# Two x tiles move into bytes that attention's far pool frees early, and stay until layer 2; the last pieces of layer 1 are split

## The chip, the cores and the metric

The kernel runs on one core of a Trainium2 chip. TensorE (PE) multiplies matrices, VectorE (DVE), ScalarE (ACT) and GpSimd (POOL) work on tiles in the on-chip memory SBUF or in the matmul accumulators (PSUM), and transfers between SBUF and the main memory (HBM) are issued from the queue of an engine: here that of SyncE (SP), or now and then that of ScalarE or GpSimd. Each engine works through its instructions in order and waits on semaphores for others. The metric is the device time of one execution in microseconds (us).

## The reference

A residual network of four layers on x of shape (1, 256, 256, 128) in float32, that is 65,536 tokens of 128 channels. Each layer gets the group-normalised x and its output is added to x:

```python
x = x + attention(gn(x))            # layer 0: triangle attention, 4 heads of 32 channels, pair bias
x = x + multiply16(gn(x))           # layer 1:
#   a = sigmoid((x@Wa1+ba1) * (x@Wa2+ba2)); b likewise, 16 channels each
#   z = einsum("bikc,bkjc->bijc", a, b)
#   out = sigmoid(x@Wg+bg) * (layernorm(z)@Wz + bz)
x = x + multiply128(gn(x))          # layer 2: zn = layernorm(x); a, b, k with 128 channels
#   out = sigmoid(zn@Wgo+bgo) * (layernorm(k)@Wlo + blo)
x = x + conv(gn(x))                 # layer 3: small convolutions and shifts
```

The group normalisation before a layer (gn0 to gn3) needs the mean and the variance of the whole x, 32 groups of four channels. So no layer can start before the last piece of the x before it is summed up.

## The kernel before

x lies channel by channel in HBM: 128 partitions by 65,536 tokens. The versions after each layer are called xT, x1T, x2T and x3T. Outside attention they are worked on in 32 tiles (NSC) of 2,048 tokens (SC), 1 MB each. Parts of the kernel are written with the order of instructions fixed by hand (manual_schedule); between the parts the instructions of one engine follow one another in the order of the program, or as the planner places them.

**Attention (layer 0)** works on 64 groups (NG) of 1,024 tokens (GT = 4 rows of 256). A loop over j (L700) takes half a group at a time: it loads x of the group after next (load_x, L482) and its normalising factors (load_rs, L487), centres and scales them to xn (centre, L496; prepare), projects xn of the next group to q, k, v and the gate (project, L514 to L536), computes the scores of this group (L545, each matmul reads a slice of k and one of q), adds the bias and takes exponentials (weigh, L559 on), multiplies with v (attend, L578), and, two or three groups later, divides, projects out (output) and writes x1T (close, L636; the store L641 is on SyncE's queue, those of the last two groups on ScalarE's). Its SBUF pools: p2, which rotates two tiles of q, k and xn each, three of v, the gate and u, and five of x; p2e for the exponentials, and p2c for the bias.

**Between the layers.** order1 (L776) is the order of the tiles in layer 1. Thirteen pools of one tile each (slots) are opened once attention's pools are closed, over the same bytes. Eight loads (FIRST, L786) are issued on SyncE's queue. gn1's statistics are merged (L790), a flag tells whether a number has overflowed (L791 to L799), the flag is read into a register of every engine (L800), and under tc.If (L801) a general attention would be computed anew and the eight tiles loaded again; this branch isn't taken. Then gn_groups (L194 to L208) turns the statistics into a mean and 1/sqrt(variance) for each channel: two small matmuls, a square root on ScalarE (L206) and a reciprocal. The factors are folded into the weights (L824 to L832).

**Layer 1.** p3 (L846 to L880) first issues the loads of slots 8 to 12 (L853), then for each tile eight matmuls (L860), an activation (L869), a product (L870), a sigmoid (L846) and the store of 0.25 MB to abD; the next load takes the slot that the tile left (load1 at L784). z (L883 to L941) multiplies a and b. p4 (L944 to L1030) takes the tiles in another order, beginning with the last twelve, which are still in the slots: gate4 computes the gate, TensorE the projection of z into PSUM (pz, one tile's two halves at a time), VectorE the product (L1008), and the sum is added to x, on GpSimd (L1019) for most tiles and on VectorE (L1015) for those of by_dve, where the product is left in PSUM until it is added. sum4 (L979 to L981) squares the new tile on ScalarE and sums it, and the tile is stored to x2T from SyncE (L1025, the last one L1030).

**Layer 2.** x_pool (x57) holds seven tiles. gn2 (L1041 to L1065) sums up the statistics and folds them in as gn1 did. load5 (L1090) loads x2 tiles, the first four on GpSimd's queue, the others on SyncE's; square5, sums5 and root5 compute the layer norm's factors, the first tile by itself; the factors of each tile go through a row in HBM (rs2D). Then each tile goes through five products (L1154), the gated a and b are stored to aD and bD, and p6, p7 and p9 follow.

Of the kernel before, what the change touches and what calls it, by code (L numbers as in the profile page):

```python
# [16 lines left out]
P = 128  # L17
N = 256
# [14 lines left out]
def kernel(ctx: ExitStack, tc: tile.TileContext, a: dict, out: bass.AP):  # L33
# [435 lines left out]


    stats1 = new_stats("stats1")
    rzD = dram.tile([N // 4, 16, N], F32, name="rzD")
# [3 lines left out]
    with tc.tile_pool(name="p2e", bufs=6, reuse_waits="tile") as eb, tc.tile_pool(name="p2c", bufs=1, reuse_waits="tile") as cs:  # L476
        triT = cs.tile([P, NH, 2, N], F32, name="triT")
        with tc.tile_pool(name="p2", bufs=2, reuse_waits="tile") as sb, tc.tile_pool(name="p2S", bufs=2, space=PSUM, reuse_waits="tile") as psS, tc.tile_pool(name="p2z", bufs=1, space=PSUM, reuse_waits="tile") as psZ, tc.tile_pool(name="p2M", bufs=3, space=PSUM, reuse_waits="tile") as psM, ExitStack() as by_hand:
            groups = {}
            rows = {}  # L480

            def load_x(g):  # L482
                x = sb.tile([P, GT], F32, name="p2_x", bufs=5)
                nc.sync.dma_start(x, xT[:, g * GT : (g + 1) * GT])
                groups[g] = dict(x=x)
# [10 lines left out]
            def centre(g):  # L496
                t = groups[g]
                t["xn"] = sb.tile([P, GT], F32, name="p2_xn")
                nc.scalar.activation(t["xn"], t["x"], AF.Identity, bias=mneg)  # L499
                return t["xn"]  # L500
# [5 lines left out]
            def tiles(g):  # L506
                t = groups[g]
                t["q"] = sb.tile([P, GT], F32, name="p2_q")
                t["k"] = sb.tile([P, GT], F32, name="p2_k")
                t["v"] = sb.tile([P, GT // P, D], F32, name="p2_v", bufs=3)  # L510
                t["g"] = sb.tile([P, GT], F32, name="p2_g", bufs=3)
                t["u"] = sb.tile([P, GT], F32, name="p2_u", bufs=3)
# [190 lines left out]
            for j in range(2 * NG + 5):  # L703
# [5 lines left out]
                if not 0 <= out[0] < NG:  # L709
                    out = None  # L710
                if j == 20:

                    pick = cs.tile([P, G, P], F32, name="pick")
                    nc.gpsimd.tensor_copy(
                        pick.rearrange("p r (h m) -> p r h m", h=NH),
                        ident.rearrange("p (h x) -> p x h", h=NH)[:, 0:G, :].unsqueeze(3).to_broadcast([P, G, NH, HC]),
                    )

                    nc.sync.dma_start(
                        sD_tap[:, 8:].rearrange("k (h w) -> k h w", w=NP)[:, :, 0:8],  # L720
                        fill[:, 0:1, :].to_broadcast([TAPS, N + 2, 8]),
                    )
                    nc.sync.dma_start(sD_tap[:, 0:8], fill[:, 0, :])
                    nc.sync.dma_start(
                        sD_tap[:, 16 : 8 + NP].rearrange("k (a w) -> k a w", w=8),
                        fill[:, 1:2, :].to_broadcast([TAPS, N // 8, 8]),
                    )
                    nc.sync.dma_start(
                        tD[:, NP : 2 * NP].rearrange("o (a w) -> o a w", w=8),
                        fill[0:1, 0:1, :].to_broadcast([1, NP // 8, 8]),  # L730
                    )
# [43 lines left out]

    order1 = [b + h * NSC // 2 for b in range(NSC // 2) for h in range(2)]  # L776
    SLOTS, FIRST = 13, 8
    x1_scope = ExitStack()
    slots = [x1_scope.enter_context(tc.tile_pool(name=f"x1_{i}", bufs=1, reuse_waits="tile")) for i in range(SLOTS)]
    xs = {}  # L780

    def load1(s, slot):
        xs[s] = slots[slot].tile([P, SC], F32, name="x1", tag="x1")
        nc.sync.dma_start(xs[s], x1T[:, s * SC : (s + 1) * SC])  # L784

    for i in range(FIRST):  # L786
        load1(order1[i], i)
# [13 lines left out]
    with tc.If(again > 0):  # L801
        general_attention(
            tc, dict(xT=xT, rsD=rsD, mbD=mbD, triD=triD, x1T=x1T),
            dict(wf=wf, wo=wo, b_g=b_g, b_o=b_o, cqkg=cqkg, cv=cv, ctri=ctri, toff=toff, mneg=mneg, ident=ident),
            dram, stats1,
        )
        nc.vector.bn_aggr(mv1, stats1.rearrange("p n s -> p (n s)"))
        for s in order1[:FIRST]:
            nc.sync.dma_start(xs[s], x1T[:, s * SC : (s + 1) * SC])
# [26 lines left out]
    usum = const.tile([P, 2 * NSC], F32, name="usum")  # L836
    qsum = const.tile([P, NSC], F32, name="qsum")

    with x1_scope:
        with tc.tile_pool(name="p3", bufs=3, reuse_waits="tile") as sb, tc.tile_pool(name="p3ps", bufs=3, space=PSUM, reuse_waits="tile") as ps, tc.manual_schedule():  # L840
# [11 lines left out]

            for i in range(FIRST, SLOTS):  # L853
                load1(order1[i], i)
            for i, s in enumerate(order1):
# [90 lines left out]
        with tc.tile_pool(name="p4", bufs=3, reuse_waits="tile") as sb, tc.tile_pool(name="p4psg", bufs=2, space=PSUM, reuse_waits="tile") as psg, tc.tile_pool(name="p4psz", bufs=2, space=PSUM, reuse_waits="tile") as psz, tc.manual_schedule():  # L946
# [3 lines left out]
            order = [order1[i] for i in (*range(20, NSC), 19, 18, *range(18))]  # L950
            by_dve = (5, 11, 17, 23, 29, NSC - 1)

# [26 lines left out]
            def sum4():  # L979
                i = sums.pop(0)  # L980
                nc.scalar.activation(  # L981
                    junk, xs[order[i]], AF.Square, bias=c1neg, accum_out=qsum[:, i : i + 1]
                )

# [5 lines left out]
            for i, s in enumerate(order):  # L990
# [32 lines left out]
                if i:  # L1023
                    s_ = order[i - 1]
                    nc.sync.dma_start(x2T[:, s_ * SC : (s_ + 1) * SC], xs[s_])  # L1025
                j = i - 4 + SLOTS
                if i > 3 and j < NSC:
                    load1(order[j], (j + 7) % SLOTS)
            sum4()
            nc.sync.dma_start(x2T[:, s * SC : (s + 1) * SC], xt)  # L1030

# [3 lines left out]
    layer0.close()  # L1035
    x_scope = ExitStack()
    x_pool = x_scope.enter_context(tc.tile_pool(name="x57", bufs=7, reuse_waits="tile"))

# [48 lines left out]
    with tc.tile_pool(name="p5", bufs=2, reuse_waits="tile") as sb, tc.tile_pool(name="p5q", bufs=4, reuse_waits="tile") as sq_pool, tc.tile_pool(name="p5psX", bufs=1, space=PSUM, reuse_waits="tile") as psX, tc.tile_pool(name="p5psM", bufs=3, space=PSUM, reuse_waits="tile") as psM, tc.manual_schedule():  # L1087
        xs, sqs, zns, vars_ = {}, {}, {}, {}

        def load5(s):  # L1090
            if s < NSC:
                xs[s] = x_pool.tile([P, SC], F32, name="p5_x", tag="x")
                (nc.gpsimd if s < KB else nc.sync).dma_start(xs[s], x2T[:, s * SC : (s + 1) * SC])

# [84 lines left out]
        for s in range(NSC):  # L1179
# [23 lines left out]
            for dst, t in zip((aD, bD), ab):  # L1203
                nc.sync.dma_start(
                    dst[:, :, :].rearrange("p c t -> c p t")[:, 4 * s : 4 * s + 4, :],
                    t.rearrange("c (p t) -> c p t", p=4),
                )
# [28 lines left out]
    def load_row7(s):  # L1236
        if s < NSC - 2:
            nc.sync.dma_start(row7(s), rs2D[:, s * SC : (s + 1) * SC])

# [4 lines left out]
    def load7x(s):  # L1244
        if s < NSC:
            xs7[s] = x_pool.tile([P, SC], F32, name="p7_x", tag="x")
            nc.sync.dma_start(xs7[s], x2T[:, s * SC : (s + 1) * SC])
# [51 lines left out]
    def load9(s, own=None, queue=nc.sync):  # L1299
        if s < NR:  # L1300
            if s % 9 not in (6, 7):
                xs9[s] = x_pool.tile([P, R, N], F32, name="p9_x", tag="x")
            else:
                xs9[s] = own.tile([P, R, N], F32, name="p9_x")
            queue.dma_start(xs9[s], x3r[:, s * R : (s + 1) * R, :])
# [170 lines left out]
    with tc.tile_pool(name="p9", bufs=2, reuse_waits="tile") as sb, tc.tile_pool(name="p9psM", bufs=2, space=PSUM, reuse_waits="tile") as psM, tc.tile_pool(name="p9psX", bufs=2, space=PSUM, reuse_waits="tile") as psX, tc.manual_schedule():  # L1476
# [247 lines left out]
        for s in range(NR + 2):  # L1724
# [44 lines left out]
            if 0 < s <= NR:  # L1769
                last = qs[s - 1][:, :, N - 1 : N]  # L1770
                nc.scalar.activation(last, last, AF.Identity, bias=kcol[:, 1:2])
        keep_out()
    x_scope.close()

# [177 lines left out]
```

## Time and profile before

| what | value |
|---|---|
| median of three runs | 3272.09 us (3267.91 to 3276.04) |
| the profiled execution | 3273.64 us, its span 3271.7 us |
| mean granted clock of TensorE | 0.965 |
| busy: TensorE, VectorE, ScalarE, GpSimd | 93%, 69%, 62%, 54% |
| attention's loop | about 245 to 1467 us, half a group in 9.40 us |
| branch, gn1 | 1487 to 1498 us |
| p3, z, p4 | 1498 to 1579, 1579 to 1641, 1622 to 1812 us |
| gn2 and layer 2's projections | 1812 to 2190 us |

Times within the profile count from the span's start. In rows of the timeline the first two numbers are the start and the busy time of a run of instructions, then come engine, line, operation, output<-inputs, shapes and count; in square brackets stands the idle time of that engine before, and what ended it. Rows of waits name who waited for what, then the total in us, the number of waits and the longest. PEq, SPq and the like are an engine's sequencer or queue.

### The profile page before, as it was taken

What the parts mean: (1) busy time and instruction counts of PE and PEld (TensorE: products, weight loads), DVE (VectorE), ACT (ScalarE), POOL (GpSimd) and SP (SyncE); (2) the same over time, 40 slices, a digit from 0 to 9 for tenths busy, and PEclk for the clock granted to TensorE, in tenths of its full rate; (3) what the DMA queues carried; (4) which work ended last, traced back from release to release, by engine and by line L of the source; (5) the groups of instructions that cost most, each with busy time, mean ns of one, the idle gap of its engine ahead of it and who ended that gap; (6) DMA issues with size and microseconds to landing.
All of it is one profiled execution on the core that took longest, in us unless ns stands there. A gap on an engine that the chain in (4) does not pass through costs nothing. (4 is left out here: it accounts for less than half of the span.)

```text
span 3271.7 us, 51718 instructions
## 1 busy us (share of the span) xinstructions
PE 3040.7 (93%) x19792; PEld 1629.4 (50%) x19792; DVE 2248.5 (69%) x2540; ACT 2033.8 (62%) x2270; POOL 1773.4 (54%) x1019
## 2 busy tenths in 40 slices
PE   5678999999999999997799799999999989979998
PEld 4524555555555555552433244444699933324444
DVE  5626888888888888883456454454455588858887
ACT  3576777777777777763467545444344457757776
POOL 4055777777777777770268000000255568848887
PEclk8899999999999999998999899999999999989999
DMA  9982333333333333329679678666699989976775
GB/s 362 363 326 94 120 113 111 118 111 111 118 111 112 120 109 116 119 100 394 227 308 410 255 255 307 256 249 262 260 351 352 351 313 388 390 286 194 233 231 154
DMA packets 294802, 749.18 MB, mean 229 GB/s; under 512 B 71127, under 2 KB 142185, under 8 KB 245369
## 3 DMA queue, kind: packets, MB, share of 16 engines
q1 hardware_dynamic: 282671, 731.12, 61.9%
q0 software_dynamic: 9040, 13.17, 1.1%
q8 instruction: 158, 2.59, 0.3%
q10 hardware_dynamic: 2840, 1.54, 0.2%
q14 instruction: 93, 0.76, 0.1%
HBM read 458.07 MB, written 287.64 MB: 228 GB/s over the span
## 5 line engine op out<-in xcount | busy, mean ns | idle before, releaser
L555 DVE TENSOR_TENSOR p_e<-p_S,triT 128x1024 f32<-128x1024 f32 x512 | 609.4, 1212 | 144.8 <-PE p_S L545 144.8
L565 POOL TENSOR_TENSOR p_es<-p_e 128x1024 f32<-128x1024 f32 x256 | 602.8, 2367 | 126.2 <-issue 66.7
L563 ACT ACTIVATE p_e<-p_e,mbT 128x1024 f32<-128x1024 f32 x512 | 552.1, 1138 | 61.6 <-DVE p_e L555 61.6
L1154 PE MATMUL p_pm<-p_zn,wf 128*128 128x512 f32 x1040 | 448.7, 593 | 1.9 <-ACT p_a L1189 1.9
L530 PE MATMUL p_mm<-p_xn,w 128*128 128x512 f32 x768 | 405.1, 611 | 0.3 <-DVE p_v L525 0.3
L1154 PEld LDWEIGHTS p_pm<-p_zn,wf 128*128 128x128 f32 x1040 | 196.8, 190 | 253.9 <-issue 247.0
L545 PE MATMUL p_S<-p_q,p_k 32*128 32x256 f32 x4096 | 295.3, 401 | 3.5 <-DVE p_e L555 3.3
L1251 POOL MEMSET k<- 128x512 f32 x1 | 0.5, 525 | 522.4 <-PE p_pm L1154 522.4
L545 PEld LDWEIGHTS p_S<-p_q,p_k 32*128 32x128 f32 x4096 | 185.8, 184 | 159.5 <-PE p_mm L521 91.7
L504 POOL TENSOR_TENSOR p_xn<-p_xn,p_rs 128x1024 f32<-128x1024 f32 x63 | 151.3, 2401 | 205.1 <-ACT p_xn L499 108.4
L1910 PE MATMUL tp_z<-p_B,tp_at 128*128 128x256 f32 x1024 | 250.8, 388 | 0.9 <-DMA p_B<-bD 0.6
L578 PE MATMUL p_o<-p_e,p_v 128*32 128x256 f32 x4096 | 248.6, 383 | 0.0
L1282 POOL TENSOR_TENSOR k<-k,p_sq 128x512 f32<-128x512 f32 x128 | 163.1, 1274 | 136.5 <-ACT p_sq L1280 136.5
L1910 PEld LDWEIGHTS tp_z<-p_B,tp_at 128*128 128x128 f32 x1024 | 185.1, 191 | 21.9 <-DVE tp_at L1901 1.6
L530 PEld LDWEIGHTS p_mm<-p_xn,w 128*128 128x128 f32 x768 | 125.9, 190 | 104.4 <-issue 88.6
L1281 DVE TENSOR_TENSOR k<-tp_z,k 128x512 f32<-128x512 f32 x128 | 88.5, 692 | 127.0 <-ACT p_sq L1280 127.0
L578 PEld LDWEIGHTS p_o<-p_e,p_v 128*32 128x32 f32 x4096 | 120.3, 110 | 110.3 <-ACT p_g L536 41.5
L1278 ACT COPY p_K<-tp_z 128x512 f32<-128x512 f32 x128 | 74.9, 585 | 155.4 <-PE tp_z L1910 155.4
L536 ACT ACTIVATE p_g<-p_mm,bgh 128x512 f32<-128x512 f32 x128 | 87.9, 687 | 131.4 <-PE p_mm L530 131.4
L1193 DVE SCALAR_TENSOR_TENSOR p_b<-p_pm,b2w,p_b 128x1024 f32<-128x1024 f32 x64 | 82.2, 1284 | 121.7 <-PE p_pm L1154 107.3
L534 ACT ACTIVATE p_k<-p_mm,cqkg 128x512 f32<-128x512 f32 x128 | 87.9, 687 | 125.1 <-PE p_mm L530 124.9
L521 PEld LDWEIGHTS p_mm<-w,p_xn 128*128 128x128 f32 x1024 | 134.4, 191 | 61.1 <-issue 60.4
(386 smaller groups left out, 6101.2 us busy)
## 6 DMA issues: line engine op xcount, KB each, us to landing
p_x<-x2T SPq DMA_DIRECT2D x60, 1024.0 KB
x<-x1T SPq DMA_DIRECT2D x51, 1024.0 KB
p_x<-in_x_dram SPq DMA_DIRECT2D x32, 1024.0 KB
p_x<-xT SPq DMA_DIRECT2D x64, 512.0 KB
x2T<-x SPq DMA_DIRECT2D x32, 1024.0 KB
aD<-p_a SPq DMA_DIRECT2D x32, 1024.0 KB
bD<-p_b SPq DMA_DIRECT2D x32, 1024.0 KB
p_A<-aD SPq DMA_DIRECT2D x32, 1024.0 KB
```

The lines of the kernel that those rows point to most:

```text
L504: nc.gpsimd.tensor_tensor(xn, xn, groups[g]["rs"], ALU.mult)
L521: nc.tensor.matmul(pm[:, k * D : (k + 1) * D], lhsT=t["xn"][:, b * P : (b + 1) * P], rhs=wf[:, 2 * D : 3 * D], start=True, stop=True,)
L530: nc.tensor.matmul(pm, lhsT=w, rhs=t["xn"][:, cs_], start=True, stop=True)
L545: nc.tensor.matmul(Ss[h // 2][:, h % 2, u, :], lhsT=t["k"][hp, r * N + u * P : r * N + (u + 1) * P], rhs=t["q"][hp, r * N : (r + 1) * N], ...
L555: nc.vector.tensor_tensor(e[:, :, 2 * p : 2 * p + 2, :].rearrange("p u h n -> p h u n"), Ss[p], triT[:, 2 * p : 2 * p + 2, :, :], ALU.add,)
L563: nc.scalar.activation(e[:, u, :, :], e[:, u, :, :], AF.Exp, bias=mbT[:, u, i : i + 1])
L565: nc.gpsimd.tensor_tensor(es, e[:, 0, :, :], e[:, 1, :, :], ALU.add)
L578: nc.tensor.matmul(t["o"][hp, r % 2, :], lhsT=t["v"][:, r * 2 + u, hp], rhs=e[:, u, h, :], start=(u == 0), stop=(u == 1),)
L1154: nc.tensor.matmul(pm[:, c, :], lhsT=wf2[:, i, :], rhs=zns[s][:, k * CK : (k + 1) * CK], start=True, stop=True)
L1281: nc.vector.tensor_tensor(k1, pz, k1, ALU.add)
L1282: nc.gpsimd.tensor_tensor(k2, k2, sq, ALU.add)
L1910: nc.tensor.matmul(pz[:, t, :], lhsT=at[:, u, t * P : (t + 1) * P], rhs=Bc[:, u, :], start=(u == 0), stop=(u == 1))
```

## The change

Four parts:

1. **Attention's tiles.** A new pool "p2f" on the second (right) side of SBUF holds the two xn tiles and one tile of q and k for the even groups; q and k are now the two halves of one tile, and that of the odd groups stays in p2. x and the constant pick get a pool of their own. At j = 126 the far pool is closed, two slot pools of one x tile are opened over its bytes, and the loads of the first two tiles of order1 are issued there, within attention.
2. **The loads ahead of the branch.** The other eleven slots are opened after attention, and all of their loads are issued before the branch; the body of the branch, which isn't taken, would reload thirteen. p3 issues none ahead of its loop.
3. **p4's end.** Tile 30 is added on VectorE rather than on GpSimd. The last tile's square is split into two halves, with a column more for the sums. The stores of tiles 30 and 31 are issued from GpSimd's queue.
4. **Layer 2.** Its ring of seven x tiles is made of the two far slots and five new pools. The far slots hold tiles 18 and 3 (by p4's order positions 19 and 20) after p4, and these are taken first, without a load; order5 is the new order, and the stores to aD and bD and the rows of rs2D follow it. The other five tiles at the start are all loaded from SyncE's queue.

```diff
@@ -468,6 +468,16 @@
+    order1 = [b + h * NSC // 2 for b in range(NSC // 2) for h in range(2)]
+    SLOTS, FAR = 13, 2
+    x_scope, x1_scope = ExitStack(), ExitStack()
+    slots = []
+    xs = {}
+
+    def load1(s, slot):
+        xs[s] = slots[slot].tile([P, SC], F32, name="x1", tag="x")
+        nc.sync.dma_start(xs[s], x1T[:, s * SC : (s + 1) * SC])
+
     stats1 = new_stats("stats1")
@@ -475,12 +485,14 @@
         triT = cs.tile([P, NH, 2, N], F32, name="triT")
-        with tc.tile_pool(name="p2", bufs=2, reuse_waits="tile") as sb, tc.tile_pool(name="p2S", bufs=2, space=PSUM, reuse_waits="tile") as psS, tc.tile_pool(name="p2z", bufs=1, space=PSUM, reuse_waits="tile") as psZ, tc.tile_pool(name="p2M", bufs=3, space=PSUM, reuse_waits="tile") as psM, ExitStack() as by_hand:
+        with tc.tile_pool(name="p2", bufs=2, reuse_waits="tile") as sb, tc.tile_pool(name="p2x", bufs=5, reuse_waits="tile") as xb, tc.tile_pool(name="p2S", bufs=2, space=PSUM, reuse_waits="tile") as psS, tc.tile_pool(name="p2z", bufs=1, space=PSUM, reuse_waits="tile") as psZ, tc.tile_pool(name="p2M", bufs=3, space=PSUM, reuse_waits="tile") as psM, ExitStack() as by_hand:
             groups = {}
             rows = {}
+            far_scope = ExitStack()
+            far = far_scope.enter_context(tc.tile_pool(name="p2f", bufs=1, side="right", reuse_waits="tile"))
             def load_x(g):
-                x = sb.tile([P, GT], F32, name="p2_x", bufs=5)
+                x = xb.tile([P, GT], F32, name="p2_x")
                 nc.sync.dma_start(x, xT[:, g * GT : (g + 1) * GT])
@@ -495,7 +507,7 @@
                 t = groups[g]
-                t["xn"] = sb.tile([P, GT], F32, name="p2_xn")
+                t["xn"] = far.tile([P, GT], F32, name="p2_xn", bufs=2)
                 nc.scalar.activation(t["xn"], t["x"], AF.Identity, bias=mneg)
@@ -505,8 +517,8 @@
                 t = groups[g]
-                t["q"] = sb.tile([P, GT], F32, name="p2_q")
-                t["k"] = sb.tile([P, GT], F32, name="p2_k")
+                qk = (sb if g % 2 else far).tile([P, 2, GT], F32, name="p2_qk", bufs=1)
+                t["q"], t["k"] = qk[:, 0, :], qk[:, 1, :]
                 t["v"] = sb.tile([P, GT // P, D], F32, name="p2_v", bufs=3)
@@ -708,9 +720,14 @@
                     out = None
+                if j == 2 * NG - 2:
+                    far_scope.close()
+                    for i in range(FAR):
+                        slots.append(x_scope.enter_context(tc.tile_pool(name=f"x1_{i}", bufs=1, side="right", reuse_waits="tile")))
+                        load1(order1[i], i)
                 if j == 20:
-                    pick = cs.tile([P, G, P], F32, name="pick")
+                    pick = xb.tile([P, G, P], F32, name="pick", bufs=1)
                     nc.gpsimd.tensor_copy(
@@ -773,17 +790,9 @@
-    order1 = [b + h * NSC // 2 for b in range(NSC // 2) for h in range(2)]
-    SLOTS, FIRST = 13, 8
-    x1_scope = ExitStack()
-    slots = [x1_scope.enter_context(tc.tile_pool(name=f"x1_{i}", bufs=1, reuse_waits="tile")) for i in range(SLOTS)]
-    xs = {}
-
-    def load1(s, slot):
-        xs[s] = slots[slot].tile([P, SC], F32, name="x1", tag="x1")
-        nc.sync.dma_start(xs[s], x1T[:, s * SC : (s + 1) * SC])
-
-    for i in range(FIRST):
+    near = [x1_scope.enter_context(tc.tile_pool(name=f"x1_{i}", bufs=1, reuse_waits="tile")) for i in range(FAR, SLOTS)]
+    slots += [near[i] for i in (10, 9, 0, 1, 2, 3, 4, 5, 6, 7, 8)]
+    for i in range(FAR, SLOTS):
         load1(order1[i], i)
@@ -805,7 +814,7 @@
         nc.vector.bn_aggr(mv1, stats1.rearrange("p n s -> p (n s)"))
-        for s in order1[:FIRST]:
+        for s in order1[:SLOTS]:
             nc.sync.dma_start(xs[s], x1T[:, s * SC : (s + 1) * SC])
@@ -834,7 +843,7 @@
     usum = const.tile([P, 2 * NSC], F32, name="usum")
-    qsum = const.tile([P, NSC], F32, name="qsum")
+    qsum = const.tile([P, NSC + 1], F32, name="qsum")
@@ -850,8 +859,6 @@
-            for i in range(FIRST, SLOTS):
-                load1(order1[i], i)
             for i, s in enumerate(order1):
@@ -948,7 +955,7 @@
             order = [order1[i] for i in (*range(20, NSC), 19, 18, *range(18))]
-            by_dve = (5, 11, 17, 23, 29, NSC - 1)
+            by_dve = (5, 11, 17, 23, 29, NSC - 2, NSC - 1)
@@ -978,9 +985,11 @@
                 i = sums.pop(0)
-                nc.scalar.activation(
-                    junk, xs[order[i]], AF.Square, bias=c1neg, accum_out=qsum[:, i : i + 1]
-                )
+                parts = [slice(0, SC)] if i < NSC - 1 else [slice(h * 2 * CK, (h + 1) * 2 * CK) for h in range(2)]
+                for h, hs in enumerate(parts):
+                    nc.scalar.activation(
+                        junk[:, hs], xs[order[i]][:, hs], AF.Square, bias=c1neg, accum_out=qsum[:, i + h : i + h + 1]
+                    )
@@ -1022,19 +1031,29 @@
                     s_ = order[i - 1]
-                    nc.sync.dma_start(x2T[:, s_ * SC : (s_ + 1) * SC], xs[s_])
+                    (nc.sync if i < NSC - 1 else nc.gpsimd).dma_start(x2T[:, s_ * SC : (s_ + 1) * SC], xs[s_])
                 j = i - 4 + SLOTS
...
             sum4()
-            nc.sync.dma_start(x2T[:, s * SC : (s + 1) * SC], xt)
+            nc.gpsimd.dma_start(x2T[:, s * SC : (s + 1) * SC], xt)
...
     layer0.close()
-    x_scope = ExitStack()
-    x_pool = x_scope.enter_context(tc.tile_pool(name="x57", bufs=7, reuse_waits="tile"))
+    x57_scope = ExitStack()
+    ring = slots[:FAR] + [
+        x57_scope.enter_context(tc.tile_pool(name=f"x57_{i}", bufs=1, reuse_waits="tile")) for i in range(7 - FAR)
+    ]
+    turns = iter(range(FAR, 3 * NSC))
+    first5 = [order[SLOTS + 6 + i] for i in range(FAR)]
+    order5 = first5 + [s for s in range(NSC) if s not in first5]
+    x2_kept = [xs[s] for s in first5]
+
+    def x_tile(shape, name):
+        return ring[next(turns) % 7].tile(shape, F32, name=name, tag="x")
+
@@ -1089,8 +1108,12 @@
             if s < NSC:
-                xs[s] = x_pool.tile([P, SC], F32, name="p5_x", tag="x")
-                (nc.gpsimd if s < KB else nc.sync).dma_start(xs[s], x2T[:, s * SC : (s + 1) * SC])
+                if s < FAR:
+                    xs[s] = x2_kept[s]
+                    return
+                xs[s] = x_tile([P, SC], "p5_x")
+                at = order5[s] * SC
+                nc.sync.dma_start(xs[s], x2T[:, at : at + SC])
@@ -1202,7 +1225,7 @@
                 nc.sync.dma_start(
-                    dst[:, :, :].rearrange("p c t -> c p t")[:, 4 * s : 4 * s + 4, :],
+                    dst[:, :, :].rearrange("p c t -> c p t")[:, 4 * order5[s] : 4 * order5[s] + 4, :],
                     t.rearrange("c (p t) -> c p t", p=4),
@@ -1235,7 +1258,8 @@
         if s < NSC - 2:
-            nc.sync.dma_start(row7(s), rs2D[:, s * SC : (s + 1) * SC])
+            at = order5.index(s) * SC
+            nc.sync.dma_start(row7(s), rs2D[:, at : at + SC])
@@ -1243,7 +1267,7 @@
         if s < NSC:
-            xs7[s] = x_pool.tile([P, SC], F32, name="p7_x", tag="x")
+            xs7[s] = x_tile([P, SC], "p7_x")
             nc.sync.dma_start(xs7[s], x2T[:, s * SC : (s + 1) * SC])
@@ -1299,7 +1323,7 @@
             if s % 9 not in (6, 7):
-                xs9[s] = x_pool.tile([P, R, N], F32, name="p9_x", tag="x")
+                xs9[s] = x_tile([P, R, N], "p9_x")
             else:
@@ -1770,6 +1794,7 @@
         keep_out()
+    x57_scope.close()
     x_scope.close()
...
```

## The prediction

> **What bounds the kernel now.** I read the windows first, by stage, then the waits and rows of the two places that the change touches. Windows (start:end; length; busy PE, PEld, DVE, ACT, POOL with counts; granted clock; DMA share; GB/s), from two answers, the first for steady attention:
>
> ```profile
> 400.00:1400.00 1000.00, 1000.00 (x10200) 556.69 (x10203) 850.33 (x905) 720.91 (x798) 751.15 (x321) 1.00 0.34 114
> ...
> 1446.00:1467.00 21.00, 19.49 (x239) 9.70 (x238) 17.30 (x20) 11.51 (x11) 11.73 (x5) 0.92 0.22 67
> 1467.00:1493.00 26.00, 9.82 (x50) 4.62 (x42) 14.51 (x22) 0.00 (x0) 4.66 (x2) 0.79 0.97 383
> 1493.00:1496.00 3.00, 0.64 (x3) 0.61 (x3) 0.69 (x4) 0.85 (x1) 0.00 (x0) 0.50 0.08 27
> 1498.00:1509.00 11.00, 11.00 (x82) 3.11 (x86) 3.20 (x6) 5.98 (x9) 0.00 (x0) 0.79 1.01 416
> 1509.00:1570.00 61.00, 48.33 (x436) 13.06 (x428) 18.78 (x25) 29.88 (x51) 0.00 (x0) 1.00 1.02 417
> 1788.00:1812.00 24.00, 9.97 (x34) 3.17 (x26) 17.10 (x28) 13.29 (x14) 14.21 (x6) 0.60 1.01 425
> ```
>
> Attention is TensorE from end to end. From 1467 on the transfers set the pace: eight x1 tiles come in at a DMA share of 0.97, then follow three nearly idle microseconds (1493 to 1496), then layer 1's projections (p3) at 1.02. The end of p4 is saturated too. Layer 2 (1842 to 2180) has TensorE busy throughout at a share of 0.75, so what its start gains or loses stays.
>
> The idle three microseconds, in the waits of SyncE's queue and the operations of the flag's branch (duration min/median/max in ns, first and last start):
>
> ```profile
> SPq L801 <- SPq L801: 6.7, 3, 5.5
> ```
>
> ```profile
> L801 SPq EVENT_SEMAPHORE  x8: 17/17/17, 1488.4 to 1495.1; - x8
> ...
> L801 PEldq COMPARE_BRANCH  x1: 6579/6579/6579, 1487.7 to 1487.7; - x1
> ```
>
> and in the timeline:
>
> ```profile
> 1493.70 0.15 DVE L835 TENSOR_SCALAR c1neg<-gn_mv 128x1 f32<-128x1 f32 x1 [6.68 <-DVEq L801]
> 1494.54 0.50 PEld L197 LDWEIGHTS gn_pm<-gn_mv,gmat 128*128 128x128 f32 x2 [8.00 <-PEq L801]
> 1495.15 1.28 ACT L206 ACT_TABLE_LOAD   x1 [28.15 <-SPq L801]
> 1498.28 2.78 PE L860 MATMUL p<-x,v 128*32 128x512 f32 x11
> ```
>
> The reader is to see two gates ending together. SyncE walks through eight semaphores; the last passes at 1495.1, just after the last of the eight loads landed (1494.98, from its transfer's row). ScalarE's root waits for that, and TensorE works 3.1 us later. TensorE itself left its branch only at 1494.31.
>
> The second place, p4's end:
>
> ```profile
> 1787.03 4.55 POOL L1019 TENSOR_TENSOR x<-x,p_g 128x2048 f32<-128x2048 f32 x1
> 1793.75 2.35 DVE L1015 TENSOR_TENSOR x<-p_pz,x 128x1024 f32<-128x1024 f32 x2
> 1796.95 1.09 POOL L1093 DMA_DIRECT2D p_x<-x2T  x2 [5.36 <-DMA x2T<-x]
> 1798.05 4.52 POOL L1019 TENSOR_TENSOR x<-x,p_g 128x2048 f32<-128x2048 f32 x1
> 1802.61 2.00 ACT L981 ACTIVATE p_junk<-x,c1neg 128x2048 f32<-128x2048 f32 x1 [8.89 <-POOL x L1019]
> 1803.07 4.53 POOL L1019 TENSOR_TENSOR x<-x,p_g 128x2048 f32<-128x2048 f32 x1
> 1809.76 2.00 ACT L981 ACTIVATE p_junk<-x,c1neg 128x2048 f32<-128x2048 f32 x1
> 1811.89 0.19 DVE L1043 TENSOR_REDUCE gn_d<-qsum 128x1 f32<-128x32 f32 x1 [3.04 <-ACT p_junk L981]
> ```
>
> GpSimd sat 5.36 us in a load's wait, so tile 28 was added late; its square waited 8.89 us, and tile 31's square ended p4.
>
> **Attention's pools: 0.** No instruction is added but two loads. Each score matmul (L545) reads both q and k of its group, so one tile for the two comes free when two came free; the rotation stays two deep, xn's too. That work hides them is the 1000.00 us of TensorE in 1000. Were the cover gone, one exposed 687 ns activation (L534) in each of 64 groups would cost 44 us. A gain is excluded while TensorE is full.
>
> **Two loads early.** The far tiles' last reader is a projection (L530) of group 63 that starts at 1445.33. SyncE's queue is free from 1445.83; its next entry is an x1T store at 1453.25. Two 1 MB loads at some 2.45 us each fit into the 1446 to 1467 window, whose share is 0.22. Nobody waits.
>
> **Eleven loads ahead of the branch instead of eight.** The first near slot now lies over v of the last groups and waits for the last attend, about 1467.8 against 1467.17; the others queue behind it on SyncE, as does the flag's load into a register, which is needed only at 1487. Three more tiles, 3.146 MB at 425.6 KB per us (p4's end, the fullest window), take 7.4 us. So the last landing goes from 1494.98 to about 1502.8 less some 0.8, since the last of eight ended in a window not full: I take 1502.0, between 1500.5 and 1504. All transfers issued before the branch are what SyncE walks through, so the first matmul of p3 comes at 1502.0 + 3.3 = 1505.3, 7.0 later than 1498.28. TensorE's branch at 1494.31 is then covered.
>
> p3 after that: before, the stream began again at 1496 and carried 24 loads and 32 stores of 0.25 MB, 33.55 MB, 78.8 us at 425.6; it ended when z's loads began, 1579.6, so 4.8 us were lost. After, the other five loads are gone, so the transfers stand still until tile 0's matmuls are done (3.7 us after the first, by the product at 1502.05) and its slot's load is issued and under way, which I put at 4.7 (1510.0). Then 19 loads and 32 stores, 28.31 MB, take 66.5, with the same 4.8 lost: 1581.3. That is **+1.7** (+0.2 to +3.7 by the landing's bounds; even at a landing of 1500.3). The two early tiles save 4.9 us of transfer, and the longer standstill eats it.
>
> Here a rule stands against the change too. The Trainium skill ("Runtime: NRT & Kernel Launch", Instruction fetch mechanics) says that a taken branch outside the current window must fetch its target by DMA before it goes on. The 6.58 us branch agrees. By that rule the fetch would stretch with more loads in flight; even doubled it would end at 1500.9, before the landing taken above, and by either the sum is the same.
>
> **p4's end.** GpSimd's queue loses the four loads (0.53 to 0.59 us each) and the 5.36 us wait, and gets two stores at the end of its work, behind which nothing of p4 is queued. Tile 28's addition follows at once: 1791.58 to 1796.1. Tile 30 goes to VectorE: its products at 1797.26 and 1798.47 stay, its two additions (2.35) end at 1802.02. They hold the psum that tile 31 needs: the first half is free at 1800.85, and 2.33 later (1794.93 to 1797.26 before) its product starts, 1803.18 instead of 1800.79. Products 2.4, additions 1805.6 to 1807.95. The square in halves, each half of 2.00 and the 0.19 that reads the sum, from 1806.9 and from 1808.1, ends near 1809.4 against 1811.86: -2.45. The mean's sums now queue behind the additions on VectorE (they began at 1805.47), +0.25. Sum **-2.2** (-3 to -1).
>
> SyncE now has five x2 loads among its last x2T stores; each waits for an older store to land, and a load took 9.1 to 13.4 us to land here. If store 29 lands after 1817, the mean's square at 1819.34 - 2.2, which lies over its slot, is late: 0 to +4. I take 0, since the stores of 1793 to 1808 have 2 MB less of loads beside them.
>
> The pages also hold a rule against the moved stores: the Trainium skill ("SBUF — State Buffer", SBUF: two separate sides) says that a DMA of the GpSimd queue has its descriptors written by GpSimd and starves while certain VectorE operations lock it out. No row here shows a starved issue; by that rule store 31 would only land later, which is the 0 to +4 above.
>
> **Two tiles kept: 0.** Before, x0 landed at 1796.2 and was needed at 1814.5; x1 at 1806.0, needed at 1821.93. No one waited, and no one is freed. The permuted rows cost nothing: the same transfers, other addresses.
>
> **Sum.** 0 + 1.7 - 2.2 + 0 = -0.5. The profiled run took 3273.64 us, 1.94 beyond its span and 1.55 above the median of 3272.09; against the median I forecast 3271.6. The measurement of this kernel tells about 0.3% (9.8 us) from no change.
>
> **The rivals.**
> - *The branch doesn't wait for the landing.* Then p3 starts near 1498.5, bound by TensorE's branch, slots come free at 1502.2 as the last load lands, and the stream never stops: 1502.5 + 66.5 + 4.8 = 1573.8, -5.8; with -2.2, -8, about 3264 (3260 to 3268). For it: the branch's own 6.58 us end with the loads. Against it: eight semaphores to 1495.1.
> - *The last landing is later still*: SyncE's loads waited 5.2 us in three waits for earlier landings before issuing, and thirteen have more such waits. Each microsecond past 1500.3 costs one; beyond 1512.5 it decides for over 0.3% slower. Middle case +8, 3280. Against it: the share of 0.97 while they waited.
> - *Attention waits after all* for a tile that comes free later: 0.08 us in each of 128 half-groups are 10 us, and from there it is slower: 3282 to 3316. Against it: the readers named above.
> - *The change does nothing where it aims*, since no x2 load was waited for: this is in the forecast.
>
> **How the numbers follow.** Forecast 0.48, own range 3267 to 3277; no waiting at the branch 0.28; later landing 0.14; attention 0.10. Faster: half of the second case and 0.04 of the first's tail, 0.18. Slower: attention, over half of the later landing, 0.03 of the first's tail: 0.21. Same 0.61. The range leaves out the far half of attention and the ends: 3260 to 3284.
>
> **What would show it.** Two loads landing by 1455; the last semaphore of the branch near 1502 and p3's first matmul 3.3 later; an idle stretch of the transfers up to 1510; z's loads near 1581; gn2's sum of squares 2.2 earlier relative to p4's start; attention's half-groups unchanged at 9.40 us. I am wrong if p3 starts before 1500, or attention grows.

## The result: slower by 0.4%, and where the time went

The changed kernel took 3284.76 us (median; 3277.76 to 3288.19) against 3269.13 us (3266.34 to 3276.07) for the kernel before; the ratio is 1.0039 with a 95% interval of 1.0029 to 1.0048. That is 9 to 16 us slower and just outside the range that was forecast.

The profiled execution has a span of 3285.8 us, 14.2 more than before. The starts of the same rows in both profiles say where they came in:

| from ... to (us) | before | changed | difference |
|---|---|---|---|
| span's start to attention's first score matmul | 262.7 | 265.6 | +2.9 |
| to the flag's matmul behind attention | 1223.3 | 1223.3 | 0 |
| to gn1's root (its table load) | 9.1 | 16.2 | +7.1 |
| to p3's first matmul | 3.1 | 3.1 | 0 |
| to p3's last product | 74.4 | 70.8 | -3.6 |
| to p4's first gate matmul | 49.5 | 48.7 | -0.8 |
| to p4's last gate matmul | 164.7 | 169.1 | +4.4 |
| to gn2's sum of squares | 24.9 | 22.7 | -2.2 |
| to layer 2's first mean square | 7.5 | 14.3 | +6.8 |
| to the end | 1452.3 | 1452.0 | -0.3 |

At the branch, the operations of its line and the timeline of the changed kernel (columns as in the views of the kernel before):

```profile
L810 SPq EVENT_SEMAPHORE  x8: 17/17/17, 1497.4 to 1505.2; - x8
...
L810 PEldq COMPARE_BRANCH  x1: 6359/6359/6359, 1490.6 to 1490.6; - x1
```

```profile
1497.32 0.50 PEld L197 LDWEIGHTS gn_pm<-gn_mv,gmat 128*128 128x128 f32 x2 [7.91 <-PEq L810]
1505.08 1.28 ACT L206 ACT_TABLE_LOAD   x1 [35.22 <-SPq L810]
1508.14 4.40 PE L867 MATMUL p<-x,v 128*32 128x512 f32 x20
...
1792.02 5.37 PE L978 MATMUL p_pg<-x,wgf 128*128 128x512 f32 x8 [1.93 <-DMA x<-x1T]
...
1803.58 2.35 DVE L1024 TENSOR_TENSOR x<-p_pz,x 128x1024 f32<-128x1024 f32 x2
...
1811.77 7.82 SPq L1116 DMA_DIRECT2D p_x<-x2T  x2
...
1819.46 0.18 DVE L1062 TENSOR_REDUCE gn_d<-qsum 128x1 f32<-128x33 f32 x1
1819.69 2.81 SPq L1034 DMA_DIRECT2D x2T<-x  x2
...
1833.80 0.69 ACT L1140 ACTIVATE p_m<-p_st,off 128x512 f32<-128x512 f32 x1 [9.63 <-DMA x2T<-x]
```

The reader is to see two things. TensorE left its branch at about 1497, but ScalarE was held until the last of the eight semaphores, 1505.2. And tile 29's additions (L1024) ended at 1805.93, but the stores of tiles 28 and 29, the last two on SyncE (L1034), left only from 1819.69 on, behind two loads (L1116); layer 2's mean square, whose tile lies over tile 29's slot, waited 9.63 us for the landing. SyncE's waits of that stretch:

```profile
SPq L1116 <- DMA x2T<-x: 33.9, 5, 15.3
```

Five x2 loads waited 33.9 us in all for older stores. The standstill of the transfers behind the branch is the middle one of these windows:

```profile
1470.00:1503.00 33.00, 10.24 (x48) 5.07 (x44) 14.67 (x24) 0.00 (x0) 4.66 (x2) 0.73 0.99 395
1503.00:1512.00 9.00, 5.39 (x40) 2.42 (x44) 1.67 (x10) 2.23 (x3) 0.00 (x0) 0.50 0.04 15
1512.00:1575.00 63.00, 53.37 (x484) 14.44 (x480) 21.67 (x29) 34.54 (x56) 0.00 (x0) 1.00 1.00 398
```

So the forecast's path was there, but a late store, a slower p4 and a later first score came on top. The experiments ask what each belongs to.

### The profile page after: what moved, and what is told of

It reads as the page before. It is cut to its first block, busy times and chain, and to the rows that moved or that the text cites. A ratio compares the mean times of both kernels' runs of the same rounds, so it can differ in the third digit from the quotient of the medians.

```text
span 3285.8 us, 51664 instructions
## 1 busy us (share of the span) xinstructions
PE 3039.5 (93%) x19792; PEld 1629.0 (50%) x19792; DVE 2247.9 (68%) x2542; ACT 2034.6 (62%) x2272; POOL 1769.1 (54%) x1016
## 5 line engine op out<-in xcount | busy, mean ns | idle before, releaser
L557 PE MATMUL p_S<-p_qk 32*128 32x256 f32 x4096 | 295.3, 401 | 3.5 <-DVE p_e L567 3.2
L557 PEld LDWEIGHTS p_S<-p_qk 32*128 32x128 f32 x4096 | 185.8, 184 | 159.5 <-PE p_mm L533 91.7
L548 ACT ACTIVATE p_g<-p_mm,bgh 128x512 f32<-128x512 f32 x128 | 87.9, 687 | 134.9 <-PE p_mm L542 134.9
L546 ACT ACTIVATE p_qk<-p_mm,cqkg 128x512 f32<-128x512 f32 x128 | 88.0, 687 | 121.6 <-PE p_mm L542 121.3
```

What stands on the lines that cost most here:

```text
L557: nc.tensor.matmul(Ss[h // 2][:, h % 2, u, :], lhsT=t["k"][hp, r * N + u * P : r * N + (u + 1) * P], rhs=t["q"][hp, r * N : (r + 1) * N], ...
```

## The experiments

Times are medians, and ratios are to the kernel before on the same chip, with their 95% intervals. The runs were made on several chips, so two runs are best compared by their ratios: 0.001 of ratio is 3.3 us, and the difference of two ratios is known to about 0.0014, or 4.6 us. A table of steps for all runs stands behind them.

**1. The x2 loads behind the stores** (on the changed kernel). The planner had put the five loads between the last stores on SyncE; here they queue behind tile 29's.

```diff
-        for s in range(7):
-            load5(s)
+        with tc.issue_after(last_put.ins):   # the store of tile 29
+            for s in range(7):
+                load5(s)
```

> The changed kernel with one thing altered: layer 2's five first x2 loads are queued on SyncE behind the store of tile 29 instead of between the stores of tiles 24 to 29. Theory Q (the queue): the loads wait for older stores to land and hold the stores behind them back, so store 29 left at 1820.85 although its additions ended at 1805.93, and layer 2's first mean square (whose tile lies over tile 29's slot) waited 9.63 us for its landing. Then here store 29 leaves within 2 us of its additions, that wait goes, the square starts about 2.7 us after the first sums as before the change, and the time falls by some 7 us to about 3278. Rival S (saturation): the transfers are full until 1834 in any order, the landing stays where it is, and the time stays at 3283 to 3286.

3277.72 us, ratio 1.0016 (1.0008 to 1.0025). The timeline of this run:

```profile
1771.34 33.68 SPq L1034 DMA_DIRECT2D x2T<-x  x8
...
1802.10 2.35 DVE L1024 TENSOR_TENSOR x<-p_pz,x 128x1024 f32<-128x1024 f32 x2
...
1805.19 5.01 SPq L1118 DMA_DIRECT2D p_x<-x2T  x5
...
1825.12 0.69 ACT L1142 ACTIVATE p_m<-p_st,off 128x512 f32<-128x512 f32 x1 [2.46 <-PE p_st L1136]
```

Tile 29's additions ended at 1804.45 and the eight stores were out before 1805.19; the mean square waited for TensorE's sums again, not for a store. Queue, not saturation: 7 us of the loss (7.5 by the ratios).

**2. Ten loads ahead of the branch** (on the changed kernel): two far and eight near; the other three follow the branch.

```diff
-    for i in range(FAR, SLOTS):
+    FIRST = 10
+    for i in range(FAR, FIRST):
         load1(order1[i], i)
...
+            for i in range(FIRST, SLOTS):
+                load1(order1[i], i)
             for i, s in enumerate(order1):
```

> The changed kernel with ten loads (two far, eight near) ahead of the branch instead of thirteen; the other three are issued after it, as five were before the change. Theory L (landing): the branch's path waits for every landing, so the last semaphore passes about 7.4 us earlier, at about 1497.5 on this profile's clock, p3's first matmul comes 3.1 us after it, the standstill of the transfers goes, and p3 ends 5 to 7 us earlier than in the changed kernel: about 3278 to 3280. Rival: the standstill is given back, as p3 and z are followed by p4 whose transfers are full anyway; then less than 2 us is gained.

3278.18 us, ratio 1.0026 (1.0016 to 1.0035). The branch's line in this run, and the window about it:

```profile
L811 SPq EVENT_SEMAPHORE  x8: 17/17/17, 1496.4 to 1496.9; - x8
```

```profile
1491.00:1498.00 7.00, 1.11 (x4) 1.00 (x4) 0.69 (x4) 1.41 (x2) 0.00 (x0) 0.50 0.44 167
```

From the flag's matmul to p3's last product it takes 82.7 us, against 90.0 in the changed kernel and 86.6 before. The landing sets the start, and the standstill is worth 7.3 us in this stretch; p4 doesn't give it back (its gates took 166.8 us against 169.1). The median fell by 6.6 us, the ratio by 4.3; in this profile attention took 3.3 us longer than in the changed kernel, all of it in its first 100 us, at a granted clock of 0.97 instead of 1.00. Its late store is still there (8.61 us of wait for it).

**3. Both together.**

> The changed kernel with both alterations, the loads behind the stores and ten loads ahead of the branch. If theories Q and L are both right and add up: some 13 us below the changed kernel, 3270 to 3272, a little above or at the time before; p4's end 2.2 us shorter than before and p3's 4.9 us should even bring 3264 if nothing else was lost. If p4's late last x1 load (1.93 us of waiting at 1792, and a slow clock behind it) belongs to the change and not to chance, about 4 us of that stays lost.

3267.87 us, ratio 0.9990 (0.9980 to 1.0000): 16.9 us under the changed kernel's median, 3.3 more than the two alone, which lies within their intervals. The whole loss is gone, and no tile has been moved back yet. p4's late load remained in it: its gates took 167.1 us against 164.7 before.

**4. The tail alone** (on the kernel before): tile 30 on VectorE, the last square in halves with qsum's 33rd column; no queue and no pool is changed.

```diff
-            by_dve = (5, 11, 17, 23, 29, NSC - 1)
+            by_dve = (5, 11, 17, 23, 29, NSC - 2, NSC - 1)
-    qsum = const.tile([P, NSC], F32, name="qsum")
+    qsum = const.tile([P, NSC + 1], F32, name="qsum")
```

> The kernel before with part 3 alone, without its queues: tile 30 added on VectorE, the last square in halves; loads and stores stay where they were. If the split by itself brings the 2.2 us: 3267. If it needs GpSimd's queue free of the load's wait of 5.4 us, tile 28's addition stays at 1798.05 to 1802.57, the four squares behind it run one after another to about 1811.6, and the time stays within 0.5 us of the kernel before, 3269.

Neither: 3278.20 us, ratio 1.0021 (1.0011 to 1.0031). A change of two instructions at p4's end cost about 7 us, and its profile shows them far from there: the first score 4.5 us later, p4's gates 3.7 us longer. What it has in common with the changed kernel is the column. It adds 4 bytes a partition, which the constants' pool rounds to 32, and every tile above the constants moves by 32 bytes: the slots begin at byte 48,160 instead of 48,128, which is 188 times 256 (these are the addresses that the built programs list).

**5. The column alone** (on the kernel before).

```diff
-    qsum = const.tile([P, NSC], F32, name="qsum")
+    qsum = const.tile([P, NSC + 1], F32, name="qsum")[:, 0:NSC]
```

> The kernel before with nothing altered but that qsum's tile is allocated with a 33rd column that nothing uses. Every SBUF tile allocated above the constants then stands 32 bytes further, off its multiple of 64 bytes, as in the changed kernel and in the run with the tail alone. Theory A (address): transfers to and from these tiles are a little slower, so the stages that transfers bound (p0, p3, p4 and those after layer 2) grow, and the time rises by about the 7.5 us that the tail alone cost, to 3276 to 3279. Rival: the place doesn't matter and the tail's own instructions cost the 7.5; then the time stays at 3270 to 3271.

3277.87 us, ratio 1.0020 (1.0011 to 1.0030). No instruction is added, taken out or moved, and 6.5 us (3.6 to 9.8) are lost. The windows of p4's 120 us from 40 us behind its first gate matmul on, first the kernel before, then this one:

```profile
1662.20:1782.20 120.00, 119.02 (x381) 44.01 (x380) 69.09 (x104) 97.96 (x97) 100.31 (x34) 0.98 0.96 383
```

```profile
1666.40:1786.40 120.00, 118.72 (x380) 43.73 (x378) 69.16 (x105) 97.77 (x97) 100.47 (x33) 0.98 0.97 375
```

The transfers are as busy (0.96 and 0.97) and carry 2% less, 375 against 383 GB/s; the busy times of the engines differ by under 1%.

Not every saturated stretch pays. These are 60 us of p3, from 8 us behind its first matmul on, first the kernel before, then this one:

```profile
1506.30:1566.30 60.00, 48.47 (x436) 13.13 (x432) 19.52 (x26) 30.40 (x52) 0.00 (x0) 1.00 1.02 419
```

```profile
1510.80:1570.80 60.00, 48.94 (x443) 13.27 (x436) 19.53 (x26) 30.96 (x52) 0.00 (x0) 1.00 1.02 420
```

The same slots are loaded, 32 bytes off in the second, at the same rate, and p3 took as long (86.4 against 86.6 us from the flag's matmul to its last product). From layer 2 on the pools begin lower, at byte 40,672 before and at 40,704, which is 159 times 256, with the column. So there the column moves the tiles onto a multiple of 256, and nothing is gained: the last stretch takes 1452.6 us against 1452.3. That the column costs time is shown, and that p4 pays a part of it; why p4 pays and p3 doesn't stays open.

**6. The tail with the 32 bytes given back** (on the kernel before): vb1 and vb2, 32 bytes each, share a tile.

```diff
-    vb1 = const.tile([P, 1], F32, name="vb1")
-    vb2 = const.tile([P, 1], F32, name="vb2")
+    vb12 = const.tile([P, 2], F32, name="vb12")
+    vb1, vb2 = vb12[:, 0:1], vb12[:, 1:2]
```

> The tail alone again, but with vb1 and vb2 in one tile, which gives the 32 bytes back: the tiles stand where they stood before. Theory A: the 7.5 us go, 3268 to 3271. Rival (the tail's own instructions): 3278 as without it.

3270.73 us, ratio 0.9999 (0.9989 to 1.0010): the loss is gone. The same window of this run:

```profile
1656.40:1776.40 120.00, 119.03 (x382) 44.01 (x379) 68.95 (x105) 97.35 (x95) 99.53 (x33) 0.98 0.96 385
```

Its p4 ends in 22.7 us like the changed kernel's, 2.2 under the kernel before, while run 4 needed 24.3. GpSimd's waits in run 4 and then in this one:

```profile
POOL p_x L1095 <- DMA x2T<-x: 6.8, 1, 6.8
```

```profile
POOL p_x L1095 <- DMA x2T<-x: 3.6, 1, 3.6
```

As these two profiles have it, the split pays as far as that wait is short. Whether its 2.2 us reach the end can't be read from a ratio with this interval.

**7 to 10. The tiles back in their places, on the changed kernel and with the repairs.** Runs 7 and 8 use the shared tile of run 6; the far slots still end at byte 229,344 and so begin 32 bytes off. Runs 9 and 10 add a gap of 992 bytes ahead of the far pool, so that all slots begin at multiples of 1024.

```diff
             far_scope = ExitStack()
+            x_scope.enter_context(tc.tile_pool(name="gap", bufs=1, side="right", reuse_waits="tile")).tile([P, 248], F32, name="gap")
```

The changed kernel with the shared tile:

> The changed kernel with vb1 and vb2 in one tile, so that all but the two far slots stand at multiples of 64 bytes again. Theory A: about 7 us less than the changed kernel's 3284.8, so 3276 to 3279, with the late store of tile 29 and the longer wait at the branch as they were. Rival: 3283 to 3286.

3281.15 us, ratio 1.0033 (1.0020 to 1.0046): 3.6 us by the medians and 2 by the ratios, where 7 were expected.

The repairs of run 3 and the shared tile:

> The changed kernel with all three: loads behind the stores, ten loads ahead of the branch, tiles back on multiples of 64 bytes. By theories Q, L and A together 3284.8 - 7 - 6.6 - 7 = 3264, or below it since the first two gave 16.9 together and not 13.6: 3259 to 3265. Without A it stays at 3268.

3266.59 us, ratio 0.9994 (0.9985 to 1.0003): 1.3 us under run 3 by the medians and 1.3 above it by the ratios, where 4 or more were expected.

The changed kernel with the gap too:

> The changed kernel with all large tiles at multiples of 1024 bytes: vb1 and vb2 in one tile as in the run before, and a gap of 992 bytes ahead of the far pool, whose slots had stood 32 bytes off still. Theory A: the part of the 7.4 us that the run with vb1 and vb2 alone did not give back (it gave 3.6) comes back too, 3277 to 3278. Rival (the far slots' place costs nothing, the rest was chance): 3281 as without the gap.

3279.24 us, ratio 1.0027 (1.0017 to 1.0037): 3.9 us under the changed kernel by the ratios (5.5 by the medians), and still behind the kernel before. What is left is what the forecast spoke of, the branch and the store:

```profile
L811 SPq EVENT_SEMAPHORE  x8: 17/17/17, 1493.0 to 1500.6; - x8
```

```profile
1500.50 1.28 ACT L206 ACT_TABLE_LOAD   x1 [35.17 <-SPq L811]
...
1823.03 0.69 ACT L1141 ACTIVATE p_m<-p_st,off 128x512 f32<-128x512 f32 x1 [7.89 <-DMA x2T<-x]
```

All three together:

> The three together, loads behind the stores, ten loads ahead of the branch, and all large tiles at multiples of 1024 bytes. Theory A for the far slots: some 2 to 4 us below the same without the gap, 3262 to 3265, and faster than the kernel before beyond the interval. Rival: 3266 to 3267.

3265.22 us, ratio 0.9991 (0.9982 to 1.0000): 14 us under run 9, as runs 1 and 2 gave singly, and some 3 us better than the kernel before, at the edge of what its interval tells. But run 3, with every tile of layer 1 32 bytes off, stood at 0.9990: in the kernel with both repairs the places brought nothing that the medians show. What the far slots' place costs by itself lies within the intervals and is left open.

**11 and 12. Which place costs** (on the kernel before): 64 and 128 bytes more of constants.

```diff
+    qsum = const.tile([P, NSC + 16], F32, name="qsum")[:, 0:NSC]    # run 11; NSC + 32 in run 12
```

> The kernel before with nothing altered but 64 bytes more of constants, so that the tiles above stand at multiples of 64 bytes that are none of 128. If the 32 bytes off a multiple of 64 were the cause of the 7.4 us: 3270 to 3271, as before. If any place off 128, 512 or 1024 bytes costs as much: 3277 to 3278.

3273.86 us, ratio 1.0012 (1.0002 to 1.0022).

> The kernel before with nothing altered but 128 bytes more of constants: the tiles above stand at odd multiples of 128 bytes. 32 bytes cost 7.4 us, 64 bytes 3.8. If a multiple of 128 is enough: 3270. If the cost of any place off 512 or 1024 bytes is what 64 bytes showed: 3274.

3274.18 us, ratio 1.0007 (0.9998 to 1.0016). So a multiple of 64 seems not to be enough, by an interval that barely leaves out no change; whether one of 128 is stays open.

**The steps in all profiles** (us, from the starts of the same rows):

| run | first score | flag's matmul to p3's last product | p4, first to last gate matmul | to gn2's sum of squares | to the mean square |
|---|---|---|---|---|---|
| tiles in their old places: before | 262.7 | 86.6 | 164.7 | 24.9 | 7.5 |
| 6 tail, 32 bytes back | 257.9 | 86.3 | 165.3 | 22.7 | 7.4 |
| 7 changed, shared tile | 258.0 | 90.8 | 166.0 | 22.7 | 13.9 |
| 9 changed, gap too | 261.1 | 88.3 | 166.0 | 22.6 | 12.6 |
| 8 repairs, shared tile | 259.2 | 82.6 | 165.7 | 22.6 | 7.5 |
| 10 repairs, gap too | 257.3 | 82.9 | 165.6 | 22.6 | 7.4 |
| 32 bytes off: changed | 265.6 | 90.0 | 169.1 | 22.7 | 14.3 |
| 1 loads behind stores | 260.5 | 90.0 | 169.2 | 22.6 | 7.2 |
| 2 ten loads | 260.6 | 82.7 | 166.8 | 22.6 | 13.3 |
| 3 both | 265.2 | 82.3 | 167.1 | 22.8 | 7.5 |
| 4 tail alone | 267.2 | 86.6 | 168.4 | 24.3 | 7.4 |
| 5 column alone | 267.1 | 86.4 | 168.2 | 24.7 | 7.4 |
| 64 off: 11 | 264.3 | 86.6 | 167.0 | 25.2 | 7.3 |
| 128 off: 12 | 260.8 | 87.9 | 166.0 | 24.5 | 7.5 |

(In runs 7 and 8 the two far slots are still 32 bytes off.) Left out are attention, 1223.2 to 1223.4 us but for 1226.6 in run 2 and 1225.1 in run 12, and the stretch from the mean square to the end, 1450.1 to 1456.4 us, which doesn't go by the places.

Means of the six in their places and the six 32 bytes off: first score 259.4 and 264.4, p4's gates 165.6 and 168.1. In p4 the two sets don't overlap, and neither do the rates of its window (381 to 385 GB/s in their places, 374 to 378 off, 376 in run 11, 382 in run 12). The first scores do overlap, with up to 4 us of scatter about a mean, and the rate of the stage before them (30 to 150 us: 398 to 411 against 393 to 404 GB/s) doesn't part the sets. The two differences, 5.0 and 2.5 us, are of the size of the column's cost in run 5, but they are too large by some 3 us: the profiled executions of the six that are off took 2.7 us more than their medians on average, those of the other six 0.1 less.

## Why the prediction was wrong, and where it was right

**The term that was missing: qsum's 33rd column.** The forecast listed the split square's instructions and left the column without a price. On the kernel before it costs about 6.5 us (runs 4 to 6). In the changed kernel its price is less sure: moving the tiles back brought 2 (run 7) and 4 us (run 9) by the ratios, with no gain at all still within the interval, and in the repaired kernel none (runs 3, 8 and 10). The changed kernel's +4.4 in p4 goes with its lower rate there (375 GB/s); that its +2.9 before the first score is of this kind is likely, but not shown. In the profile before, the signs were only the saturated windows; which bytes the tiles have is in no view of it.

**The term that was put at nothing: the late store.** The forecast named it ("if store 29 lands after 1817 ... 0 to +4. I take 0"). It was 6.8, the largest loss that a run took out of the changed kernel by itself. The reason given, 2 MB less of loads beside the stores, looked at the bytes; but each of the five loads waited for an older store to land, the next store stood behind that load, and the next load waited for a store that had thus left late. Run 1 undid the order alone and got 7 us, and the wait for the store went. The order of SyncE's instructions in the changed kernel is in no view of the one before, but that loads which wait for stores share a queue with stores was in the text, and the bound of 4 us had no row behind it.

**Right in its mechanism, low in its size: the branch.** Forecast: the first p3 matmul 7.0 us later, by the landing of eleven loads, and p3's end +1.7 (0.2 to 3.7). Measured: 7.0 later from the flag's matmul on, p3's end +3.4; the four profiles with thirteen loads have +1.7 (run 9) to +4.2 (run 7), 3.2 on average. The forecast took 425.6 KB per us for p3, the rate of p4's end; the changed kernel carried 408 from 1515 to 1575 us, the kernel before 417 from 1509 to 1570. Run 2 shows the cause of the later start. The rival in which the branch doesn't wait is refuted, and so is the landing later still: the last semaphore passed at 1505.2, and less the 2.9 of the start that is 1502.3, where the landing was forecast for 1502.0.

**Right: p4's end.** Forecast -2.2; measured -2.2 (24.9 to 22.7), with tile 28's addition early and GpSimd without its wait. The two stores on its queue landed after a median of 9.4 us, the four loads that were there before after 11.6, so no starving shows.

**Right: attention and the kept tiles.** From the first score to the flag's matmul both kernels take 1223.3 us, so the rival of a wait in every half-group is refuted, although the measured 3284.76 us lies in the range that was given to it (3282 to 3316): the number alone would have pointed at the wrong cause. For the two kept tiles no effect was forecast. They may be what allows the x2 loads to go late, as they do in run 1; no run tells.

**The sum.** Forecast -0.5. With the store's 6.8, the branch's 1.7 more and the column's 2 to 6.5 put in, it is +10 to +14.5, and the ratio has 9.5 to 15.7. That it closes proves no single term, and in one place it closes badly: the ratio of run 9 (5.6 to 12.1 us) lies above the 4.5 that its branch, tail and store make up (1.7 - 2.3 + 5.1).

## What to carry to other kernels

Look at what an edit does to the addresses of tiles that it doesn't touch: a column more in a small constant moved every large tile, which cost 6.5 us on the kernel before and slowed the transfers of one of its saturated stages, so it is worth comparing a kernel that has the new layout and nothing else before a loss is put down to instructions. A load that waits for a store to land belongs behind the stores on its queue, or on another queue: ahead of them it holds back what the next load waits for. And a load issued ahead of a branch is awaited by the branch, so issue as many as land by the time that the other engines are through it anyway: of the eight, ten and thirteen tried here that was ten.

## What the runs showed of the hardware that was not expected

With the tiles up to layer 1 32 bytes off a multiple of 1024 the kernel before was 0.20% (0.11 to 0.30) slower without an instruction more, with 64 bytes 0.12% (0.02 to 0.22), with 128 bytes 0.07% (-0.02 to 0.16). In p4 the same busy share of the transfers carried 375 instead of 383 GB/s; in p3 it carried 420 and 419.

The Trainium skill ("DMA: Bandwidth & Descriptors", How a descriptor splits into AXI transactions) says that a transfer's run of bytes is cut at multiples of 256 bytes, so that one that doesn't start there needs a transaction more and fetches bytes that it doesn't use. For a run of 8,192 bytes that is, as an estimate from that page, 33 transactions in place of 32, about 3%. The 2% of p4 agrees in order of size; p3, which lost nothing, doesn't. That the cost falls from 32 over 64 to 128 bytes is not what the page's count of fetched bytes would give (32, 64 and 128 unused bytes) either, though the intervals overlap.

TensorE's way through the branch took 6.3 to 6.9 us in the profiles with eight, ten and thirteen loads issued ahead of it (6.6 to 6.9 with eight, 6.5 to 6.7 with ten, 6.3 to 6.4 with thirteen), so it did not grow with them, as the forecast had thought possible.
